# Seven block products in layer 0, a planner that prefers held banks, and layer statistics on ScalarE in a four-layer graph network

## The chip, the cores and the metric

The kernel runs on one core of one Trainium2 chip. The time is the device time of one execution in microseconds. Time before: 1353.37 us, the median of 3 runs (1351.7 to 1353.72). Each run also has a profile of one execution; its span goes from the first to the last instruction of the program.

## The reference

x has 64 samples of 256 nodes with 128 features (fp32), adj is 256 x 256. Four layers follow each other, each with a residual and a layer norm over the features:

```python
x = layernorm(x + L0(x))   # sum over k of adj^k x W_k, k = 0..3 (two equal adjacencies: their weights add)
x = layernorm(x + adj @ (x @ W1) + b1)
x = layernorm(x + norm(adj + I) @ x @ W2.T + b2)
x = layernorm(x + L3(x))   # 5 steps of a gated unit:
#   m = adj @ h;  z = sigmoid(m W34 + h U3);  r = sigmoid(m W4 + h U3)
#   v = tanh(m W5 + (r * h) U5);  h = (1 - z) * h + z * v
```

Layer 0 is folded: with q = a2 x (a2 is adj squared), the layer is x(W0 + I) + q W2 + adj (x W1 + q W3), where W1, W2, W3 are sums of two raw weights each. `w0s` holds these four matrices, centred over the output features so that the layer norm needs no mean.

## The kernel before, in words

Samples go in groups of two (NB = 2), 32 groups in all. A group's tile is 128 x 512: two samples times two halves of the nodes times 128 features. All work is recorded as operations with an engine, a cost, a lag and a rank (the group's number); nothing is issued while recording. `Plan.order` (from L74) then goes through them like a scheduler: on each engine it takes the operation that can start first by these costs, among equals the one of the lowest rank, hands out tile slots ("bank" is one of 8 PSUM banks, "w" an SBUF tile of 128 x 512, and so on) and returns the order. The program is issued in that order, and each engine runs its own queue in order. At most ACTIVE groups (10) are open at a time.

Names that matter for what follows:

- `propagate` multiplies by an adjacency. For all but the first two groups' layer 0 it is `seven` (L590 on): a 2 x 2 block product with 7 instead of 8 products of 128 columns. GpSimd makes differences of the input (ts01, ts2, ts3; L614, L618, L621). TensorE does `first` (one product into quadrant 0), `middle` (three), `more` (one into quadrant 0, after ScalarE has copied that quadrant to `us`, L655) and `rest` (two). VectorE adds up (post11 to post2, L642 to L652).
- `record` (from L732) is a group's whole program. Layer 0: x is loaded; for the first two groups (`near`, HEAD = 4 samples) TensorE transposes it, for the others VectorE transposes 32 x 32 blocks (tx) and two DMAs through DRAM finish it (dx, xT). q comes from `propagate`. Then for each node half `first` does four matmuls of 256 columns (xT by the first two matrices of w0s, or of its row-permuted copy w0p, and qT by the last two), ScalarE copies one half of the bank to v (L771), `second` adds two matmuls of 256 columns with adj, and ScalarE copies the sum out (L783).
- The five steps of layer 3 are `product` calls of 512 columns each: pr (W4 and U3), gate r, r times h on VectorE, ph (W5), pr turned into z's by w34, gate z, ph (U5), gate h, then VectorE's d, e and the new hT, which `packed` sends through DRAM into the other layout (th, dh, h).
- `spread_of` and `normalise_centred` are the layer norm where the mean is zero: ScalarE squares with an accumulated sum (L515), GpSimd adds EPS and takes the power -0.5 (L519, L520), ScalarE scales (L531). `statistics` and `normalise` are layer 3's, with the mean: VectorE's bn_stats and bn_aggr (L491, L495), GpSimd (L501, L502), ScalarE (L551). The last three groups (END = 6 samples) end in `closing` instead, which lets TensorE transpose and centre, and then uses `spread_of`.
- In the set-up, w0_raw becomes w0s (sums on VectorE, then the centring); aTp is adj with its rows interleaved, made by four DMAs (`spread`, L317); `block_sums` (L355 to L359) makes for each adjacency the five block combinations that `seven` needs; p_an is the transpose of the normalised adjacency on TensorE.

All matmuls of these parts go through `mm` at L199, so the profile's groups are told apart by tiles: pmq, pm and pmg are the propagations of layers 0, 1 and 2, and 3; py is layer 0's products and the weights of layers 1 and 2; pr and ph are layer 3's.

Of the kernel before, what the change touches and what calls it, by code (L numbers as in the profile page):

```python
# [13 lines left out]
P = 128  # L14
NB = 2
ACTIVE = 10
# [34 lines left out]
class Plan:  # L51
# [32 lines left out]
    def order(self):  # L84
# [14 lines left out]
        while any(ready.values()):  # L99
            best = None  # L100
            for e, waiting in ready.items():
                t0 = free.get(e, 0.0)
                pick = None
                for at, op in waiting:
                    need = {}
                    for v in placed[op]:
                        if v.slot is None:
                            need[v.kind] = need.get(v.kind, 0) + 1
                    short = False
                    for k, n in need.items():  # L110
                        if len(pool[k]) < n:
                            short = True
                            break
                        at = max(at, sorted(pool[k])[n - 1][0])
                    if short:
                        continue
                    key = (max(at, t0), op.rank, op.seq)
                    if pick is None or key < pick[0]:
                        pick = (key, op)
# [3 lines left out]
            (start, _, _), op = best  # L123
# [34 lines left out]
def kernel(  # L158
# [42 lines left out]
    SHAPES = {"bank": [P, 512], "x": [P, 512], "w": [P, 512], "th": [P, 384], "q": [P, P], "st": [P, Q * 6], "mv": [P, Q * 2],  # L201
              "ve": [P, Q], "rs": [P, Q]}
    slots = {"bank": BANKS, "x": ACTIVE + 3, "w": 48, "th": 10, "q": 10, "dram1": 8, "dram2": 16, "st": 12, "mv": 12, "ve": 24, "rs": 12}
# [18 lines left out]
    def fetch(rank, o, src, v, queue, after=()):  # L222
        e, cost = QUEUES[queue]
        return pre(rank, queue, cost, lambda: e.dma_start(o, src), [], [v], lag=3000, joint=True, after=after)

    def load(rank, name, shape, src, keep=True, queue="SP"):
        v = constant(name, shape) if keep else Val("w", shape, name)
        e, cost = QUEUES[queue]
        pre(rank, queue, cost, lambda: e.dma_start(v.ap, src), [], [v], lag=3000 if queue != "SP" else 2300)
# [5 lines left out]
    nc.vector.memset(half, -0.5)  # L235

# [45 lines left out]
    w0_raw = load(-1, "w0_raw", [P, C, K0], w0)  # L282
# [21 lines left out]
    w0p = constant("w0p", [P, 2, C])  # L304

    def permuted():
        for r in range(4):
            nc.sync.dma_start(w0p.ap.rearrange("(j r) k c -> r j k c", r=4)[r], w0s.ap[32 * r:32 * (r + 1), 0:2, :])

    pre(1.2, "SP", 1800, permuted, [w0s], [w0p])  # L310
# [32 lines left out]
    pre(0.3, "DVE", 600, rows, [ahat, dinv], [ahat])  # L343
    pre(0.3, "PE", 4 * 110, lambda: turn(p_an, ahat), [ahat], [p_an])
# [34 lines left out]
    raw = {name: load(0.6, f"raw_{name}", [P, src.shape[1]], src, False, "SP")  # L379
# [60 lines left out]
    class Group:  # L440
# [44 lines left out]
        def statistics(self, tag, s):  # L485
            st, mv, ve, rs, nm = (self.val(k, n + tag) for k, n in (
                ("st", "st"), ("mv", "mv"), ("ve", "ve"), ("rs", "rs"), ("ve", "nm")))

            def stats():
                for q in range(self.q):  # L490
                    nc.vector.bn_stats(st.ap[:, q * 6:(q + 1) * 6], nat(s)[:, q, :])  # L491

            def aggr():
                for q in range(self.q):
                    nc.vector.bn_aggr(mv.ap[:, 2 * q:2 * q + 2], st.ap[:, q * 6:(q + 1) * 6])  # L495
                mean, var = (mv.ap.rearrange("p (q k) -> p k q", k=2)[:, k] for k in range(2))
                nc.vector.tensor_scalar(ve.ap, var, EPS, None, op0=OP.add)
                nc.vector.tensor_scalar(nm.ap, mean, -1.0, None, op0=OP.mult)

            def scales():  # L500
                nc.gpsimd.tensor_tensor(rs.ap, ve.ap, half[:, :self.q], op=OP.pow)  # L501
                nc.gpsimd.tensor_tensor(mv.ap[:, :self.q], nm.ap, rs.ap, op=OP.mult)  # L502

            self.dve(stats, [s], [st], 195 * self.q)
            self.dve(aggr, [st], [mv, ve, nm], 67 * self.q + 240)
            self.add("POOL", 1300, 100, scales, [ve, nm], [rs, mv])
            return mv, rs

        def spread_of(self, tag, s):
# [3 lines left out]
            def squares():  # L513
                for q in range(self.q):
                    nc.scalar.activation(nat(y)[:, q, :], nat(s)[:, q, :], AF.Square, scale=C ** -0.5,  # L515
                                         accum_out=ve.ap[:, q:q + 1])

            def scales():
                nc.gpsimd.tensor_scalar(ve.ap, ve.ap, EPS, None, op0=OP.add)  # L519
                nc.gpsimd.tensor_tensor(rs.ap, ve.ap, half[:, :self.q], op=OP.pow)  # L520

            self.act(squares, [s], [y, ve], 295 * self.q)
            self.add("POOL", 1330, 100, scales, [ve], [ve, rs])
# [22 lines left out]
        def normalise(self, tag, s, mv, rs):  # L546
            y = self.val("w", "y" + tag)

            def run():
                for q in range(self.q):  # L550
                    nc.scalar.activation(nat(y)[:, q, :], nat(s)[:, q, :], AF.Identity, bias=mv.ap[:, q:q + 1],  # L551
                                         scale=rs.ap[:, q:q + 1])

            self.act(run, [s, mv, rs], [y], 390 * self.q)
            return y

# [36 lines left out]
        def seven(self, tag, h, aTs, ins, blocks):  # L593
# [32 lines left out]
            def first():  # L626
                block(0, ins(h)[:, 0, 0], aTs.ap[:, 0, :P], True)

            def middle():
# [24 lines left out]
            started = self.pe(pe_cost(P, 1), first, [h, aTs], [ps])  # L654
            kept = self.act(lambda: nc.scalar.copy(row(u, 1), row(ps, 0)), [ps], [u], 165)  # L655
# [3 lines left out]
            self.pe(pe_cost(P, 3), middle, [ts, sums], [ps], True, (started,))  # L659
# [39 lines left out]
        def packed(self, name, src):  # L699
# [13 lines left out]
            self.add("SP", 900, 2300, run, [far], [t])  # L713
# [5 lines left out]
        def gate_(self, name, ps, func, bias, kept=True):  # L719

            t = self.val("w", name) if kept else ps
# [10 lines left out]
        def record(self):  # L732
            x_ = self.val("x", "x")
            plan.add("SP", 450, 4500 if self.start < HEAD else 2700, self.rank() - 1.5, lambda: nc.sync.dma_start(nat(x_), self.view(x)), [], [x_],
# [3 lines left out]
            if near:  # L738
                xT, w01 = self.copied("xT", self.transposes("x", x_)), w0s
            else:  # L740

                w01 = w0p
                turn, far = self.val("w", "tx"), self.val("dram", "dx")
                xT = self.val("w", "xT")
                self.dve(lambda: nc.vector.transpose(  # L745
                    turn.ap.rearrange("p (r b i t) -> p r b t i", r=4, t=T, i=32),
                    x_.ap.rearrange("p (b t r j) -> p r b t j", r=4, t=T, j=32)), [x_], [turn])
# [9 lines left out]
            v, s0 = self.val("w", "v"), self.val("w", "s0")  # L757
            py = []

            for t in range(T):  # L760
                p = self.val("bank", f"py0{t}")
                py.append(p)

                def first(p=p, t=t):
                    for b in range(self.nb):
                        o = p.ap[:, b * 2 * C:(b + 1) * 2 * C]
                        mm(o, (tiles if near else pairs)(xT)[:, b, t], w01.ap[:, 0:2, :], b == 0, True, shared=True)
                        mm(o, tiles(qT)[:, b, t], w0s.ap[:, 2:4, :], False, True, shared=True)

                def moved(p=p, t=t):  # L770
                    nc.scalar.copy(parts(v)[:, t], four(p)[:, :, 1, :])  # L771

                self.pe(pe_cost(2 * C, 2 * self.nb), first, [xT, qT, w01, w0s], [p])
                self.act(moved, [p], [v], 55 + 107 * self.nb)
            for t in range(T):

                def second(p=py[t], t=t):
                    for kt in range(T):
                        mm(four(p)[:, :, 0, :], aT.ap[:, kt, t * P:(t + 1) * P], parts(v)[:, kt],
                           False, True, shared=True)  # L780

                def summed(p=py[t], t=t):
                    nc.scalar.copy(nat(s0).rearrange("p (b t) c -> p t b c", t=T)[:, t],  # L783
# [129 lines left out]
```

## Time and profile before

| | |
|---|---|
| median of 3 runs | 1353.37 us (1351.7 to 1353.72) |
| the profiled execution | 1352.22 us, span 1350.3 us |
| granted TensorE clock | 0.999 |
| VectorE's largest group, rh (L729) | 160 of 767 ns |
| ScalarE's squares (L515) | 396 of 299 ns, with 396 accumulator reads of 191 ns |
| GpSimd's power (L520) | 99 of 1052 ns |
| DMA | 134.96 MB, mean 100 GB/s |

A group of the profile names line, engine, operation, output <- input, shapes and count, then busy time, mean of one in ns, the idle time of the engine just before, and what ended it. A wait is given as engine, tile and line, then who was waited for: us in total, times, longest. An ACTIVATE with an accumulated sum stands as two instructions, the second an accumulator read.

### The profile page before, as it was taken

The numbers are of one execution on the slowest core, as the hardware profiler recorded it, in microseconds if no ns is written. First come the engines' busy times: TensorE is split into PE (matmuls) and PEld (weight loads), VectorE is DVE, ScalarE is ACT, GpSimd is POOL, SyncE is SP. The second block draws the span as 40 slices with busy tenths as digits, with TensorE's granted clock in tenths as the row PEclk, the third lists the DMA queues.
The fourth block names the chain that finished last, engine by engine and source line by source line (L and its number), as shares of the span: only waits on it lengthen the run. The fifth ranks groups of instructions, "written<-read, shape, count | busy, mean of one in ns | idle before, by whom it ended". The sixth has DMA issues, their size and how long they took to land.

```text
span 1350.3 us, 22012 instructions
## 1 busy us (share of the span) xinstructions
PE 1336.5 (99%) x6553; PEld 928.3 (69%) x6553; DVE 940.9 (70%) x2304; ACT 758.1 (56%) x2421; POOL 680.7 (50%) x1097
## 2 busy tenths in 40 slices
PE   8999999999999999999999999999999999999997
PEld 7886666676776766677666666676776776565554
DVE  5466677767667667865676776676666677877776
ACT  4675536467654556556565554474655686444445
POOL 5785425266742566247266443383653686233323
PEclk9999999999999999999999999999999999999999
DMA  6322334242522333333233433341332223333323
GB/s 175 109 71 71 94 94 128 77 128 78 147 78 77 111 95 118 115 106 100 64 110 110 127 100 98 94 137 56 110 102 63 82 85 121 87 106 95 93 78 110
DMA packets 269495, 134.96 MB, mean 100 GB/s; under 512 B 175776, under 2 KB 241056, under 8 KB 269376
## 3 DMA queue, kind: packets, MB, share of 16 engines
q1 hardware_dynamic: 269120, 133.42, 34.1%
q8 instruction: 53, 0.87, 0.3%
q14 instruction: 66, 0.54, 0.1%
q0 software_dynamic: 256, 0.13, 0.1%
HBM read 67.31 MB, written 65.80 MB: 99 GB/s over the span
## 4 chain that ended last, share of the span: by engine, by line
PE 95%; DVE 1%; DMA 1%; ACT 1%; issue 0%; SPq 0%; POOLq 0%; ACTq 0%; POOL 0%; DVEq 0%
PE pr L199 31%; PE ph L199 20%; PE pmg L199 19%; PE py L199 15%; PE pm L199 7%; PE pmq L199 3%; DMA x<-in_x_dram 1%; DMA w_raw<-in_L_gnn_weight_dram 0%; PE s L199 0%; DMA dx<-tx 0%; ACT y L515 0%; ACT y L551 0%; DVE s L543 0%; SPq L748 0%; DVE tx L745 0%
## 5 line engine op out<-in xcount | busy, mean ns | idle before, releaser
L199 PE MATMUL pr<-mg,w435u5T 128*128 128x512 f32 x640 | 319.8, 593 | 0.0
L614 POOL TENSOR_TENSOR tsg<-h 128x256 f32<-128x256 f32 x128 | 97.2, 760 | 292.5 <-DMA h<-dh 197.5
L722 ACT ACTIVATE r<-pr,bsum 128x512 f32<-128x512 f32 x160 | 109.7, 685 | 151.5 <-PE pr L199 150.7
L722 ACT ACTIVATE pr<-pr,bsum 128x512 f32<-128x512 f32 x160 | 105.5, 660 | 112.4 <-PE pr L199 109.3
L729 DVE TENSOR_TENSOR rh<-r,hT 128x512 f32<-128x512 f32 x160 | 122.7, 767 | 61.6 <-ACT r L722 60.7
L199 PE MATMUL ph<-rh,w435u5T 128*128 128x512 f32 x320 | 163.6, 594 | 0.0
L199 PE MATMUL ph<-mg,w435u5T 128*128 128x512 f32 x320 | 163.3, 592 | 0.0
L199 PE MATMUL pr<-hT,w2u3T 128*128 128x512 f32 x320 | 163.0, 593 | 0.0
L729 DVE TENSOR_TENSOR d<-ph,hT 128x512 f32<-128x512 f32 x160 | 109.7, 686 | 76.1 <-ACT ph L722 73.0
L199 PEld LDWEIGHTS pr<-mg,w435u5T 128*128 128x128 f32 x640 | 109.4, 191 | 65.3 <-issue 53.3
L722 ACT ACTIVATE ph<-ph,bsum 128x512 f32<-128x512 f32 x160 | 105.6, 660 | 60.4 <-PE ph L199 59.9
L531 ACT ACTIVATE y<-s,rs 128x128 f32<-128x128 f32 x384 | 122.1, 392 | 11.0 <-POOL rs L520 10.7
L515 ACT ACTIVATE y<-s 128x128 f32<-128x128 f32 x396 | 116.7, 299 | 16.9 <-DVE s L538 14.9
L199 PEld LDWEIGHTS pmg<-s_aTp,tsg 128*128 128x128 f32 x768 | 101.8, 192 | 33.5 <-issue 28.5
L652 DVE TENSOR_TENSOR mg<-pmg,usg 128x256 f32<-128x256 f32 x160 | 67.0, 419 | 72.7 <-PE pmg L199 70.4
L199 PEld LDWEIGHTS pmg<-aTp,h 128*128 128x128 f32 x512 | 87.1, 197 | 39.4 <-issue 29.2
L729 DVE TENSOR_TENSOR pr<-pr,d 128x512 f32<-128x512 f32 x157 | 108.7, 692 | 1.5
L520 POOL TENSOR_TENSOR rs<-ve,half 128x4 f32<-128x4 f32 x99 | 104.1, 1052 | 8.3
L519 POOL TENSOR_SCALAR ve<-ve 128x4 f32<-128x4 f32 x99 | 23.2, 234 | 166.6 <-ACT y L515 166.3
L729 DVE TENSOR_TENSOR hT<-hT,pr 128x512 f32<-128x512 f32 x157 | 106.1, 676 | 1.3
L199 PE MATMUL pmg<-s_aTp,tsg 128*128 128x128 f32 x768 | 106.2, 275 | 0.0
L642 DVE TENSOR_TENSOR usg<-usg,pmg 128x128 f32<-128x128 f32 x160 | 45.2, 284 | 81.7 <-PE pmg L199 47.7
(181 smaller groups left out, 2816.9 us busy)
## 6 DMA issues: line engine op xcount, KB each, us to landing
dh<-th SPq DMA_DIRECT2D x160, 256.0 KB, 2.0
h<-dh SPq DMA_DIRECT2D x256, 128.0 KB, 2.5
x<-in_x_dram SPq DMA_DIRECT2D x32, 256.0 KB, 3.4
hT<-dh SPq DMA_DIRECT2D x128, 64.0 KB, 2.0
out_dram<-y SPq DMA_DIRECT2D x32, 256.0 KB, 2.3
dx<-tx SPq DMA_DIRECT2D x30, 256.0 KB, 2.6
xT<-dx SPq DMA_DIRECT2D x60, 128.0 KB, 2.6
dn<-tn SPq DMA_DIRECT2D x29, 256.0 KB, 2.1
```

Source lines behind the costliest of these rows:

```text
L199: nc.tensor.matmul(o, lhsT, rhs, start=start, stop=stop, skip_group_check=shared)
L515: nc.scalar.activation(nat(y)[:, q, :], nat(s)[:, q, :], AF.Square, scale=C ** -0.5, accum_out=ve.ap[:, q:q + 1])
L519: nc.gpsimd.tensor_scalar(ve.ap, ve.ap, EPS, None, op0=OP.add)
L520: nc.gpsimd.tensor_tensor(rs.ap, ve.ap, half[:, :self.q], op=OP.pow)
L531: nc.scalar.mul(nat(y)[:, q, :], nat(s)[:, q, :], rs.ap[:, q:q + 1])
L614: nc.gpsimd.tensor_tensor(ts.ap[:, :2 * P].rearrange("p (x c) -> p x c", x=2), ins(h)[:, 1], ins(h)[:, :, 0], op=OP.subtract)
L642: nc.vector.tensor_tensor(row(u, 0), row(u, 1), row(ps, 3), op=OP.add)
L652: nc.vector.tensor_tensor(o(m, slice(1, 3)), o(ps, slice(1, 3), False), both, op=OP.add)
L722: self.act(lambda: nc.scalar.activation(t.ap, ps.ap, func, bias=bias[1], scale=1.0), [ps, bias[0]], [t], act_cost(self.width) + 100)
L729: self.dve(lambda: nc.vector.tensor_tensor(out(t), way(a), way(b), op=op), [a, b], [t])
```

## The change

Six things change together.

1. Layer 0 of all but the first two groups becomes `inner_seven`. The 2 x 2 block matrix of the four weights is multiplied in 7 block products of 128 columns for each of the two samples (14 matmuls) instead of 8 matmuls of 256 columns. VectorE makes the differences and sums of xT and qT (s1 to s4) and adds up the products (five additions); ScalarE makes one copy (u1) and half of the result. It holds two banks. The weights' combinations w0t are made once on VectorE, and the row-permuted copy w0p with its four DMAs goes. `inner` is the old way, for the first two groups.
2. `Plan.order` gets a second key: among operations that can start at the same time, one that holds a bank already goes before one that does not. ACTIVE becomes 12; "w" slots become 38, "th" and "q" 12, and there are 21 slots of a new kind "h" (128 x 256).
3. Gate r is written to a PSUM bank instead of an SBUF tile.
4. Layer 3's `statistics` go from VectorE to ScalarE: a pass with an accumulated sum, a pass of squares with the negative mean as bias and an accumulated sum; GpSimd makes the scalings.
5. In `spread_of`, EPS enters as a bias of the squares (a 128 x 1 tile `root`) and GpSimd's addition goes.
6. `seven`'s `first` and `middle` become one step `opening` of four products, and the copy of quadrant 0 comes after all four. Costs and lags of loads are set anew, and two set-up steps (rows of ahat, the transpose p_an) get later ranks.

```diff
-ACTIVE = 10
+ACTIVE = 12
...
-                    need = {}
+                    need, opens = {}, 1
                     for v in placed[op]:
                         if v.slot is None:
                             need[v.kind] = need.get(v.kind, 0) + 1
+                        elif v.kind == "bank":
+                            opens = 0
...
-                    key = (max(at, t0), op.rank, op.seq)
+                    key = (max(at, t0), opens, op.rank, op.seq)
...
-    w0_raw = load(-1, "w0_raw", [P, C, K0], w0)
+    w0_raw = load(-1, "w0_raw", [P, C, K0], w0, lag=7300)
...
-    pre(0.3, "DVE", 600, rows, [ahat, dinv], [ahat])
-    pre(0.3, "PE", 4 * 110, lambda: turn(p_an, ahat), [ahat], [p_an])
+    pre(0.9, "DVE", 600, rows, [ahat, dinv, w0s], [ahat])
+    pre(1.1, "PE", 4 * 110, lambda: turn(p_an, ahat), [ahat], [p_an])
...
+            def means():
                 for q in range(self.q):
-                    nc.vector.bn_stats(st.ap[:, q * 6:(q + 1) * 6], nat(s)[:, q, :])
+                    nc.scalar.activation(nat(y)[:, q, :], nat(s)[:, q, :], AF.Identity, accum_out=sums.ap[:, q:q + 1])
...
+            def squares():
                 for q in range(self.q):
-                    nc.vector.bn_aggr(mv.ap[:, 2 * q:2 * q + 2], st.ap[:, q * 6:(q + 1) * 6])
...
+                    nc.scalar.activation(nat(y)[:, q, :], nat(s)[:, q, :], AF.Square, bias=nm.ap[:, q:q + 1],
+                                         accum_out=sums.ap[:, q:q + 1])
...
                     nc.scalar.activation(nat(y)[:, q, :], nat(s)[:, q, :], AF.Square, scale=C ** -0.5,
-                                         accum_out=ve.ap[:, q:q + 1])
+                                         bias=root[:, 0:1], accum_out=ve.ap[:, q:q + 1])
 
             def scales():
-                nc.gpsimd.tensor_scalar(ve.ap, ve.ap, EPS, None, op0=OP.add)
...
+        def inner_seven(self, xT, qT):
...
+            self.add("DVE", 450, 400, s3, [xT], [sd])
+            self.add("DVE", 450, 400, s1, [xT, qT], [ss])
+            self.add("DVE", 450, 400, s2, [xT, ss], [st_])
+            self.add("DVE", 450, 400, s4, [qT, st_], [sf])
+
+            def opening():
+                times(half(out_, 0), at(xT, 0), w0s.ap[:, 0, :], True)
+                times(half(more, 0), whole(st_), w0t.ap[:, 1, :], True)
+                times(half(more, 1), whole(ss), w0t.ap[:, 0, :])
...
+            self.pe(pe_cost(P, 3 * NB), opening, [xT, ss, st_, w0s, w0t], [out_, more])
+            self.act(lambda: nc.scalar.copy(u1.ap, out_.ap[:, :N]), [out_], [u1], 270)
+            self.pe(pe_cost(P, NB), lambda: times(half(out_, 0), at(qT, 0), w0s.ap[:, 2, :]), [qT, w0s], [out_])
+            self.pe(pe_cost(P, NB), lambda: times(half(out_, 1), at(qT, 1), w0t.ap[:, 3, :]), [qT, w0t], [out_])
+            add(lambda: (u2.ap, u1.ap, more.ap[:, :N]), [u1, more], [u2])
+            self.pe(pe_cost(P, NB), lambda: times(half(more, 0), whole(sd), w0t.ap[:, 2, :]), [sd, w0t], [more])
...
+            self.pe(pe_cost(P, NB), lambda: times(half(more, 1), whole(sf), w0s.ap[:, 3, :]), [sf, w0s], [more])
...
-            started = self.pe(pe_cost(P, 1), first, [h, aTs], [ps])
-            kept = self.act(lambda: nc.scalar.copy(row(u, 1), row(ps, 0)), [ps], [u], 165)
             self.add("POOL", 830, 100, ts01, [h], [ts])
             self.add("POOL", 610, 100, ts2, [h, ts], [ts])
             self.add("POOL", 590, 100, ts3, [h, ts], [tq])
-            self.pe(pe_cost(P, 3), middle, [ts, sums], [ps], True, (started,))
+            self.pe(pe_cost(P, 4), opening, [h, ts, aTs, sums], [ps])
+            kept = self.act(lambda: nc.scalar.copy(row(u, 1), row(ps, 0)), [ps], [u], 165)
             self.pe(pe_cost(P, 1), more, [h, aTs], [ps], True, (kept,))
...
-                r = self.gate_(f"r{s}", pr, AF.Sigmoid, rb)
+                r = self.gate_(f"r{s}", pr, AF.Sigmoid, rb, "bank")
```

## The prediction

> **What bounds it now.** I read the page's busy shares first, then the waits of TensorE, then its timeline.
>
> ```profile
> PE 1336.5 (99%) x6553; PEld 928.3 (69%) x6553; DVE 940.9 (70%) x2304; ACT 758.1 (56%) x2421; POOL 680.7 (50%) x1097
> PEclk9999999999999999999999999999999999999999
> PE 95%; DVE 1%; DMA 1%; ACT 1%; issue 0%; SPq 0%; POOLq 0%; ACTq 0%; POOL 0%; DVEq 0%
> ```
>
> TensorE (PE) is busy 99% of the span at the full granted clock, and it is 95% of the chain that ended last. But ends of matmuls are modelled, so "busy" proves little; starts do. This is TensorE's timeline (start, us, line, tiles, shapes, count; an fp32 matmul stands as two instructions):
>
> ```profile
> 705.01 1.02 PE L199 MATMUL pr<-hT,w2u3T 128*128 128x512 f32 x2
> 705.87 1.02 PE L199 MATMUL ph<-mg,w435u5T 128*128 128x512 f32 x2
> 706.72 0.39 PE L199 MATMUL pmg<-aTp,h 128*128 128x128 f32 x2
> 706.95 0.39 PE L199 MATMUL pm<-s_anT,y 128*128 128x128 f32 x2
> 707.17 0.39 PE L199 MATMUL pm<-s_anT,tq 128*128 128x128 f32 x2
> 707.40 0.39 PE L199 MATMUL pm<-s_aT,y 128*128 128x128 f32 x2
> 707.62 0.39 PE L199 MATMUL pm<-s_aT,tq 128*128 128x128 f32 x2
> 707.84 1.03 PE L199 MATMUL py<-v,aT 128*128 128x256 f32 x4
> 708.71 1.02 PE L199 MATMUL pr<-mg,w435u5T 128*128 128x512 f32 x2
> ```
>
> Start to start, an instruction of 512 columns takes 0.43 us (705.01 to 705.87, two of them), one of 256 takes 0.217 (707.84 to 708.71, four), one of 128 takes 0.112 (706.72 to 707.84, ten, each pair with weights of its own). The groups by shape count 1606, 792 and 4155 of them: 690.5 + 171.7 + 466 = 1328 us. The first matmul starts at 1.4 and the last ends at 1343.4, 6.9 before the span does. 1328 + 1.4 + 6.9 = 1336; the other 14 us are matmuls that start later than this pace. So the kernel is one stream of matmuls: what shortens it is fewer columns, fewer late starts, a shorter tail. The late starts that are plain waits:
>
> ```profile
> PE warm L247 <- POOL ident masks.py:199: 1.4, 1, 1.4
> PE pmq L199 <- ACT mq L664: 1.3, 1, 1.3
> PE p_an L259 <- DVE ahat L334: 1.2, 1, 1.2
> PE pm L199 <- DVE m L648: 1.0, 2, 0.7
> PE py L199 <- DVE m L652: 0.6, 1, 0.6
> ```
>
> They and four smaller ones sum to 6.8 us. Adding up over the timeline how far each start lags the pace, 8.2 us of the 14 lie in the first 100 us and 5.4 in the 1240 after them.
>
> **1. The block products of layer 0: -9.7 us.** For 30 of the 32 groups the eight matmuls of 256 columns (16 instructions, py<-w0p,xT and py<-w0s,mq) become fourteen of 128 (28 instructions); the second stage keeps its four of 256. Removed: 30 x 16 x 0.217 = 104.2 us. Added: 30 x 28 x 0.1125 = 94.5 us (0.112 to 0.113 over the run). All of it lies on the stream, so -9.7. The weight loads double, but the same shape already runs 4155 times at 0.112 with a new weight each. The Trainium skill ("TensorE: Matmul & The Clock Gate", section "Wait — 56ns, not 53.3ns?") speaks of a fixed 2.5 ns per matmul beside its columns. By that a 128 would be half of (216.6 - 2.5) plus 2.5 = 109.5 ns, and the saving about 12; the row has 112, and the row decides.
>
> The additions around the products go to VectorE: nine of 256 elements per group (like L652, 0.42 us long, 0.34 apart), 30 x 9 x 0.34 = +92 us, less 29 x 1.2 = 35 for the removed bn_stats and bn_aggr. ScalarE loses two of four copies (0.27 apart, -16). VectorE goes from 70% to about 74%, hidden under TensorE unless it comes late at one place.
>
> **2. Statistics on ScalarE: nothing in the middle, something at the end.** A pair of ACTIVATE and accumulator read is 0.29 apart (L515 at 22.25, 22.54, 22.83). A per-partition operand adds 0.093: y<-s,mv,rs (L551) is 0.385 apart, y<-s,rs (L531) 0.292. So a group's sums cost 4 x 0.29 = 1.17 us, its squares up to 4 x 0.385 = 1.54; 29 x 2.7 = 79 us. The bias that replaces the added EPS in the other 99 normalisations costs at most 396 x 0.093 = 37, and takes 99 x 0.29 from GpSimd, where the new scalings add about 29 x 0.5. ScalarE goes from 56% to some 63%. A square with a bias alone is not in the trace: between 0.29 and 0.385; I take 0.385, the row with a bias.
>
> The gate r kept in PSUM moves ScalarE's write to the form of the in-place gates (660 against 685 ns) and VectorE's read to a PSUM one (d: 686, against rh: 767): gain off the path. The permuted copy of w0 (four DMAs, SP 13.0 to 15.4) goes; SP's next issue waits for VectorE's tx until 21.6 anyway: nothing.
>
> **3. The head: -1.4 us (bounds -3.6 to +2.0).**
>
> ```profile
> 8.23 0.60 PE L674 MATMUL ptx<-ident,x 128*128 128x128 f32 x4
> 10.03 0.81 PE L259 MATMUL p_an<-ident,ahat 128*128 128x128 f32 x4 [1.20 <-DVE ahat L334]
> 10.68 0.60 PE L674 MATMUL ptx<-ident,x 128*128 128x128 f32 x4
> 11.11 3.62 PE L199 MATMUL pmq<-a2T,x 128*128 128x256 f32 x16
> 14.57 0.59 PE L199 MATMUL py<-w0s,xT 128*128 128x256 f32 x2
> ```
>
> p_an moves behind the first layer-0 products, so its 1.5 us of lateness goes. What is late next is w0s: in the changed order VectorE makes the block sums of aT and a2T, then w0's sums, then **the block sums of aTp, and only then centres w0s**. aTp comes by four DMAs issued from 9.2 to 11.1, landing 2.1 to 3.0 later: 13.2 to 14.1. Then 1.07 (the same five instructions at 18.47 to 19.54) and 1.53 (the centring, 10.15 to 11.68): w0s is ready at 15.8 to 16.7, and the products start there, not at 14.57, with p_an's 0.45 still to do: +1.7 to +2.6, I take 2.0. TensorE stands some 3 us there. Against that, behind 14.57 the old head still loses 5.4 (8.2 less 1.5 for p_an and 1.3 at matmuls that run cold at 1 to 8 us, which stay); most are results of x loads that TensorE reaches too soon (the 1.3 at 27.8). TensorE now comes 2 us later, while VectorE's first tx starts at about 19.6 (the centring's end near 16.0 and 3.6 us of small rows), not at 20.9: I keep 2.0 of 5.4. 2.0 - 3.4 = -1.4. Keeping none gives -3.4 (-3.6 with the earliest aTp), keeping all +2.0.
>
> **4. The middle: -0.8 us (bounds -5.4 to +2.1).** 5.4 are lost now. The new order lets a step that already holds a bank go before one that opens one, and has 12 groups open, not 10; that can remove up to all. ScalarE's queue now holds 224 long blocks (squares, scalings); the change adds 58 and lengthens 99 by a third, in all 40% more; if losses go with them, +2.1. Half way, 4.6, is -0.8.
>
> **5. The tail: +2.0 us (bounds +0.7 to +2.6).** VectorE used to take the statistics of the last plain group beside ScalarE. Now ScalarE's last queue is: squares of one group (1.54), sums of group 56 (1.17), gates z and h of group 62, squares 60, a scaling (1.54), squares 56 (1.54), squares 62. The gates used to start at 1339.05 and 1339.90; now at about 1339.75 and 1340.3. Squares 60 end at 1342.4, the scaling at 1343.9, squares 56 at 1345.4, squares 62 at 1346.8, where they ended at 1344.6. GpSimd's last chain is 0.3 shorter, but takes group 56's scaling first: +2.0 net. With no price for the bias +0.7; with TensorE held up by gate h +2.6.
>
> **Sum.** -9.7 - 1.4 - 0.8 + 2.0 = -9.9. The profiled execution took 1352.2 (span 1350.3), inside the runs of 1351.7 to 1353.7 with median 1353.4: 1342.3 by the one, 1343.5 by the other. I say 1342.5. All bounds at once give -18.0 to -3.0; they are unlikely to fall together, and the range stops short below.
>
> **Rivals.** (a) Late starts vanish almost wholly and the head ends at its best: -9.7 - 3.6 - 5 + 1.5 = -17, about 1335. For it: the lags of loads are set nearer to the 4 to 7 us measured. Against: w0s. 6%. (b) ScalarE's queue takes back the gain: in each seven-product step the second matmul on quadrant 0 ("more") must wait until ScalarE has copied that quadrant. The copy takes about 0.2 + 0.27 + 0.1 us after the product. Before, the copy could run beside three further products; now all four come first. In the changed order 84 of 254 such steps have 0.9 us or less of matmuls between, formerly 25: 0.3 us to spare, less than one gate (0.57) or a block of squares (1.5). At 0.1 us lost per each of 84, 1351; **at 0.15 us it decides for slower than before**, at 0.2, 1359. Against: the same tight steps now lose next to nothing (pm <- ACT us, 0.4 in all). 9%, a third of it slower. (c) It doesn't do what it says: narrow products are not cheaper. In the busy column a 128 alone, like pmg<-aTp,h, stands at 99.5 / 512 = 0.194: 28 x 0.194 against 16 x 0.297 is +0.68 per group, +20 in all and 1372. Against: the pace 706.72 to 707.84. 3%.
>
> **The chances.** The forecast has 82%. What a measurement can tell from no change is 0.2%, 2.7 us: below 1350.7 counts as faster. From the forecast 0.80 is faster and 0.02 same, (a) gives 0.06, (b) 0.04 faster, 0.02 same, 0.03 slower, (c) 0.03 slower: 0.90, 0.04, 0.06. The range 1336.5 to 1348.5 takes in bounds of head, middle and tail short of their extremes, and leaves out (a)'s far part, (c) and most of (b).
>
> **What would show it.** Products of layer 0 as 28 instructions of 128 at 0.112; TensorE idle near 13 to 16 us waiting for VectorE's w0s; plain waits behind 100 us at about 5; last squares starting about 2 us after the last matmul. It is wrong if "more" waits on ScalarE's copies add up to over 8 us, or if matmuls lag the pace without a wait.

## The result, and the profile after

The changed kernel took 1345.13 us (median of 4 runs, 1344.37 to 1345.65) against 1353.55 us for the kernel before in the same comparison (4 runs, 1351.7 to 1354.08). The ratio is 0.994, with a 95% interval of 0.9923 to 0.9957. So it is faster by 8.4 us; forecast were 9.9 us and 1342.5. The time lies in the range given (1336.5 to 1348.5).

The profiled execution of the changed kernel took 1345.65 us with a span of 1343.9. It is the slowest of its four, 0.5 above their median, and the profiled execution of before (1352.22) lies 1.3 below its own. Between the two traces there are therefore 6.4 us of span, not 8.4, and the account below is one of 6.4.

From the page of the changed kernel, the busy shares, the granted clock and the chain that ended last:

```profile
PE 1324.9 (99%) x6913; PEld 929.7 (69%) x6913; DVE 1013.8 (75%) x2289; ACT 845.2 (63%) x2825; POOL 648.8 (48%) x1056
...
PEclk9999999999999999999999999999999999999999
...
PE 95%; DVE 2%; ACT 1%; DMA 1%; issue 0%; POOL 0%; SPq 0%; POOLq 0%; DVEq 0%; ACTq 0%
```

Nothing changed in kind. TensorE has 360 instructions more (30 groups times 12) and still fills the span; VectorE went from 70% to 75% and ScalarE from 56% to 63%. TensorE's timeline in the middle, with layer 0's seven products (start, us, line, tiles, shapes, count):

```profile
505.19 0.61 PE L201 MATMUL pz<-w0t,se 128*128 128x128 f32 x4
505.64 0.61 PE L201 MATMUL pz<-w0t,ss 128*128 128x128 f32 x4
506.09 0.39 PE L201 MATMUL pm<-aT,y 128*128 128x128 f32 x2
506.31 0.64 PE L201 MATMUL py<-w0s,xT 128*128 128x128 f32 x4
```

From 505.19 to 506.31 there are ten instructions in 1.12 us: 0.112 each (pz and py<-w0s are layer 0's). This is the pace at which the narrow products were costed. The waits of TensorE, longest first:

```profile
PE py L201 <- DVE w0s L303: 5.1, 1, 5.1
PE pmq L201 <- DVE mq L757: 1.5, 1, 1.5
PE warm L252 <- POOL ident masks.py:199: 1.4, 1, 1.4
PE pm L201 <- ACT us L767: 0.6, 1, 0.6
```

The first is new and is the longest in either of the two traces. It is what the account turns on. I made that account from the start times of all matmuls: the pace is the sum of instructions by shape times their usual distance in that trace (about 0.430, 0.216 and 0.112 us), late is what each start lags behind it, and the tail is what the span goes on after the last matmul ends. The rows add up to 1.7 less than the span, most of it the 1.4 us before the first matmul, the same in both traces. All in us:

| | before | predicted change | after | measured change |
|---|---|---|---|---|
| pace | 1328.1 | -9.7 | 1318.3 | -9.8 |
| late, first 100 us | 8.2 | -1.4 | 13.1 | **+4.9** |
| late, the rest | 5.4 | -0.8 | 1.7 | -3.7 |
| tail | 6.9 | +2.0 | 9.15 | +2.3 |
| span | 1350.3 | -9.9 | 1343.9 | -6.4 |

The products and the tail came as worked out, the middle gave more, and the head took what the middle gave. The head, in TensorE's timeline of the changed kernel:

```profile
10.95 1.89 PE L201 MATMUL pmq<-a2T,x 128*128 128x256 f32 x8
17.90 0.94 PE L201 MATMUL py<-w0s,xT 128*128 128x256 f32 x2 [5.06 <-DVE w0s L303]
18.64 1.06 PE L201 MATMUL py<-w0s,mq 128*128 128x256 f32 x2
...
21.20 0.79 PE L201 MATMUL py<-w0s,xT 128*128 128x256 f32 x2
21.82 0.59 PE L201 MATMUL py<-w0s,mq 128*128 128x256 f32 x2
```

Two things are to be seen. The products start at 17.90, not at 14.57. And from 17.90 to 21.20 the eight instructions of 256 columns take 0.41 us each, while from 21.82 on it is 0.216. The table of stretches says why (length, busy time of each engine, then the granted clock, the DMA share and GB/s):

```profile
14.00:18.00 4.00, 0.10 (x1) 0.13 (x2) 3.31 (x9) 0.00 (x0) 1.49 (x2) 1.00 0.45 133
18.00:22.00 4.00, 4.00 (x11) 3.23 (x12) 3.92 (x10) 0.37 (x1) 2.17 (x5) 0.57 0.00 0
22.00:26.00 4.00, 4.00 (x20) 3.51 (x20) 2.72 (x5) 0.84 (x3) 0.00 (x0) 1.00 0.29 85
```

After five idle microseconds the granted clock is 0.57 over the next four, then 1.00 again. The Trainium skill ("TensorE: Matmul & The Clock Gate", section "What's actually happening") says that TensorE's clock falls to half after at least one idle window of about 3.4 us and comes back after at least one busy window as long. This trace agrees: 5.06 us idle, then 3.3 us at half pace. How idle such a window has to be is read from all the traces in the last section.

VectorE's timeline shows what TensorE waited for:

```profile
9.64 0.39 DVE L292 TENSOR_TENSOR w0s<-w_raw,ident 128x128 f32<-128x128 f32 x1 [0.25 <-DMA w_raw<-in_L_gnn_weight_dram]
9.94 1.00 DVE L294 TENSOR_TENSOR w0s<-w_raw 128x128 f32<-128x128 f32 x3
14.59 0.29 DVE L364 TENSOR_TENSOR s_aTp<-aTp 128x128 f32<-128x128 f32 x1 [3.65 <-DMA aTp<-aT]
...
15.66 0.68 DVE L301 TENSOR_REDUCE w0m<-w0s 128x4 f32<-128x512 f32 x1
...
16.58 1.17 DVE L303 TENSOR_TENSOR w0s<-w0s,w0m 128x512 f32<-128x512 f32 x1
```

The sums of w0s were made at 10.9. The centring (L301 to L303) needs nothing else, but in VectorE's queue it stands behind the block sums of aTp, which is not needed until layer 3 (TensorE first uses it at 107.5). VectorE stands 3.65 us for a load that nobody wants yet.

### The profile page after: what moved, and what is told of

The parts are those of the page before. It is cut to its first block, busy times and chain, and to the rows that moved or that the text cites. A ratio compares the mean times of both kernels' runs of the same rounds, so it can differ in the third digit from the quotient of the medians.

```text
span 1343.9 us, 22953 instructions
## 1 busy us (share of the span) xinstructions
PE 1324.9 (99%) x6913; PEld 929.7 (69%) x6913; DVE 1013.8 (75%) x2289; ACT 845.2 (63%) x2825; POOL 648.8 (48%) x1056
## 4 chain that ended last, share of the span: by engine, by line
PE 95%; DVE 2%; ACT 1%; DMA 1%; issue 0%; POOL 0%; SPq 0%; POOLq 0%; DVEq 0%; ACTq 0%
PE pr L201 30%; PE ph L201 20%; PE pmg L201 19%; PE py L201 11%; PE pm L201 7%; PE pz L201 4%; PE pmq L201 3%; DVE tx L852 0%; DMA x<-in_x_dram 0%; ACT y L559 0%; ACT y L504 0%; ACT y L525 0%; PE warm L252 0%; PE s L201 0%; DMA out_dram<-y 0%
## 5 line engine op out<-in xcount | busy, mean ns | idle before, releaser
L831 ACT ACTIVATE r<-pr,bsum 128x512 f32<-128x512 f32 x160 | 105.1, 657 | 92.9 <-PE pr L201 84.7
L525 ACT ACTIVATE y<-s,root 128x128 f32<-128x128 f32 x396 | 153.7, 393 | 12.5 <-DVE s L547 11.6
L201 PEld LDWEIGHTS pr<-mg,w435u5T 128*128 128x128 f32 x640 | 106.6, 191 | 55.6 <-issue 42.5
L838 DVE TENSOR_TENSOR rh<-r,hT 128x512 f32<-128x512 f32 x160 | 109.2, 683 | 40.6 <-ACT r L831 37.4
L201 PEld LDWEIGHTS pmg<-aTp,h 128*128 128x128 f32 x512 | 91.3, 196 | 66.4 <-issue 39.7
L872 POOL TENSOR_TENSOR yb<-y,wb 128x512 f32<-128x512 f32 x64 | 82.2, 1284 | 39.9 <-ACT y L540 37.9
L201 PE MATMUL pmg<-aTp,h 128*128 128x128 f32 x512 | 99.2, 279 | 0.0
L201 PEld LDWEIGHTS ph<-rh,w435u5T 128*128 128x128 f32 x320 | 57.7, 190 | 57.5 <-issue 42.5
```

The source lines that it names most:

```text
L201: nc.tensor.matmul(o, lhsT, rhs, start=start, stop=stop, skip_group_check=shared)
L831: self.act(lambda: nc.scalar.activation(t.ap, ps.ap, func, bias=bias[1], scale=1.0), [ps, bias[0]], [t], act_cost(self.width) + 100)
L838: self.dve(lambda: nc.vector.tensor_tensor(out(t), way(a), way(b), op=op), [a, b], [t])
L872: nc.gpsimd.tensor_tensor(nat(yb), nat(y), bias[1][:, None, :].to_broadcast([P, self.q, C]), op=OP.add)
```

## The experiments

**Theory.** The net gain is that of the narrow products alone. The other parts cancel: the head loses about 5 because VectorE makes the sums of aTp before it centres w0s, and because the idle time halves TensorE's clock afterwards; the middle gains because the order prefers held banks; the tail loses 2 because ScalarE makes the statistics of the last plain groups. **Rivals:** that the head's lateness comes from the loads and the order as a whole, so that moving one step only moves the wait; that the second key in the order is not what helps the middle; that the time of the kernel is not sensitive to the tail. Kernels named together share a chip and the runs of the kernel before on it: 1354.93 us for e1 to e4, 1354.56 for e0, e5, e8 and e9, 1354.24 for e6, e7, e11 and e12. Compared are the ratios to it.

| run | ratio, 95% interval | pace | late, first 100 | late, rest | tail |
|---|---|---|---|---|---|
| e0, the changed kernel again | 0.9941, 0.9928 to 0.9955 | 1318.3 | 15.3 | 1.4 | 9.2 |
| e1 | 0.9936, 0.9923 to 0.9948 | 1318.3 | 13.9 | 1.4 | 9.15 |
| e2 | 0.9934, 0.9922 to 0.9947 | 1318.3 | 13.6 | 3.0 | 6.6 |
| e3 | 1.0, 0.9991 to 1.0009 | 1327.6 | 12.2 | 1.9 | 9.4 |
| e4 | 0.9939, 0.9926 to 0.9951 | 1322.7 | 9.0 | 1.7 | 9.15 |
| e5 | 1.0066, 1.0053 to 1.0079 | 1318.4 | 14.15 | 20.2 | 6.6 |
| e6 | 0.9968, 0.9956 to 0.9981 | 1318.5 | 14.7 | 4.8 | 9.4 |
| e7 | 0.9941, 0.9928 to 0.9953 | 1318.2 | 14.35 | 3.5 | 7.1 |
| e8 | 0.9907, 0.9893 to 0.992 | 1318.3 | 8.9 | 1.6 | 9.2 |
| e9 | 0.9898, 0.9885 to 0.9912 | 1318.3 | 8.5 | 1.4 | 9.2 |
| e11 | 1.0087, 1.0074 to 1.0101 | 1318.3 | 14.1 | 22.5 | 6.6 |
| e12 | 0.989, 0.9875 to 0.9905 | 1318.3 | 10.65 | 1.7 | 6.8 |

The columns of the account are of one profiled execution each; the head differs by one to two microseconds between executions of the same order (the first product of layer 0 starts at 17.9 in the changed kernel, at 19.0 in e0, at 18.3 in e2).

**e3: eight products again.** Is the gain the products'?

```diff
-            s0 = (self.inner if near else self.inner_seven)(xT, qT)
+            s0 = self.inner(xT, qT)
```

(and `inner` reads xT through the permuted view for the later groups).

> The changed kernel with layer 0 of all groups in the old way: 8 matmuls of 256 columns and 4 with adj, no additions on VectorE; the rest of the change stays. Theory (the gain is columns at the issue pace): 28 instructions of 0.1123 become 16 of 0.216 in 30 groups, +9.5 us of pace, and the late starts stay within 2 us of the changed kernel's: 1353 to 1357. Rival (the gain is the new order of the plan, and the products paid nothing): 1343 to 1348.

The time is that of the kernel before, 1.0 (0.9991 to 1.0009). The pace is 9.3 longer than the changed kernel's, while its late starts and tail stay within a microsecond each. So everything else in the change sums to nothing that can be measured (the interval is 1.2 us to either side), and the products, with their additions on VectorE, carry the whole net gain.

**e1: the sums of aTp right behind the centring.** Is it this one step of VectorE?

```diff
+        ops = plan.order()
+        ops.remove(early_sums)
+        ops.insert(ops.index(centred) + 1, early_sums)
-        for op in plan.order():
+        for op in ops:
```

> The changed kernel, with aTp's block sums issued on VectorE right behind the centring of w0s instead of ahead of it; all else keeps its order. Theory (w0s waits in VectorE's queue behind sums that wait for aTp's DMAs): w0s is ready at about 12.6 us (w_raw lands near 9.7, then 1.3 for its sums and 1.6 for the centring), TensorE's first layer-0 product starts at 13 to 14 instead of 17.9, none of the next eight instructions takes 0.427 us. That is 4 to 5 us of idle and 1.7 us of slow pace, 6; later waits for x loads take back 1 to 4, since VectorE's tx still stand behind the sums: 1340 to 1343. Rival (w_raw's late landing, 9.6 against 8.4, makes w0s late): the first product moves by at most 1 us, 1344 to 1345.5.

The wait for w0s went: in e1's timeline of TensorE the products start at 13.97, at full pace. But the time did not move. A little later, also from its timeline:

```profile
13.97 0.67 PE L201 MATMUL py<-w0s,xT 128*128 128x256 f32 x2
...
34.50 0.76 PE L201 MATMUL pmq<-s_a2T,x 128*128 128x128 f32 x2 [4.98 <-DVE mq L757]
35.05 0.63 PE L201 MATMUL pmq<-s_a2T,tqq 128*128 128x128 f32 x2
```

and VectorE's, which made it wait:

```profile
26.77 1.13 DVE L852 STREAM_TRANSPOSE tx<-x 128x512 f32<-128x512 f32 x1 [2.68 <-DMA x<-in_x_dram]
...
29.94 0.29 DVE L364 TENSOR_TENSOR s_anT<-anT 128x128 f32<-128x128 f32 x1
30.26 1.24 DVE L365 TENSOR_TENSOR s_anT<-s_anT,anT 128x128 f32<-128x128 f32 x1
```

The same five microseconds stand 20 us further on, again with half the pace behind them (the two instructions of 128 columns from 34.50 on take 0.55, where 0.22 is usual). VectorE first stands for a load of x and then makes the block sums of anT, needed only in layer 2, ahead of the additions of q that TensorE wants next. The theory was right on what held w0s and wrong on what its removal is worth: here the first rival's picture held, and the wait moved.

**e8: both block sums later.** The sums of aTp and of anT go behind VectorE's first s1.

```diff
+        place = next(o for o in ops if o.engine == "DVE" and any(v.name == "s1_0" for v in o.vals))
+        for o in (norm_sums, early_sums):
+            ops.remove(o)
+            ops.insert(ops.index(place) + 1, o)
```

> The changed kernel with the block sums of aTp and of the normalised adjacency (anT) both issued on VectorE behind the first addition of layer 1, at about 43 us; TensorE first needs them at 90 and 50. Theory (the head is set by VectorE's queue: once w0s is early, the next wait is for the additions of q behind these sums): TensorE's first product at 13 to 14.5, its wait for mq near 30 us 1 to 2.5 us instead of the 5.0 that the earlier swap left, no half pace behind it, late starts in the first 100 us 7 to 10 us; 2 to 5 us under the changed kernel of this chip. Rival (the x loads alone set the head, the sums are free): late starts stay at 12 to 14, time within 1 us.

Now the gain stays: late starts of the head are 8.9 instead of 15.3 in e0, and the median is 4.5 below e0's on the same chip (1342.04 against 1346.57). The account shows more than the medians, since e0's profiled execution is the slowest of its runs and e8's the fastest. The products start at 12.61:

```profile
12.61 0.67 PE L201 MATMUL py<-w0s,xT 128*128 128x256 f32 x2
13.12 0.59 PE L201 MATMUL py<-w0s,mq 128*128 128x256 f32 x2
```

**e9: e8, and two loads of x earlier.** On SP's queue x_8 and x_10 go ahead of the transfer dx_4.

```diff
+        for n in ("x_10", "x_8"):
+            ops.remove(load[n])
+            ops.insert(ops.index(load["x_6"]) + 1, load[n])
```

> As the last, and the loads of x for groups 8 and 10 issued on SP right behind that of group 6, ahead of the write of tx of group 4, behind which they stand for 8 us in the queue. Theory: their tx no longer stop VectorE for 2.5 us near 24, the additions of q start at about 27, TensorE does not wait near 30 for more than 0.5 us: 1 to 3 us under the last. Rival (landing of the others is pushed back by the two more loads in the air, or TensorE then waits for ScalarE and GpSimd in the same place): within 0.7 us of the last.

1340.89, 1.2 below e8. The four runs of e9 all lie below the four of e8, but the intervals of the ratios overlap and the account has only 0.4 us of it, so the loads' part is likely, not shown. e8 and e9 together show that most of the changed head's lateness was the place of ten small VectorE instructions: with them out of the way the head (8.5) is near before's 8.2.

**e4: TensorE kept busy in the wait.** Is the half pace a consequence of the idle time? Forty transposes into a bank that is free (p_at's) stand between the last product of q and the first of layer 0.

```diff
+            if gap:
+                for i in range(40):
+                    nc.tensor.transpose(p_at.ap[:, (i % 4) * P:(i % 4 + 1) * P], ident, ident)
```

> The changed kernel, with 40 more 128-column transposes into a finished bank issued on TensorE in its wait for w0s (about 4.4 us of work whose result nobody reads). Theory (the first eight instructions behind the wait take 0.427 us instead of 0.216 since TensorE had stood idle for 5 us): the first product still starts at 17.5 to 18.2, all instructions behind it at 0.216: -1.7 us there, part of it taken back by the waits at 34 to 39 us that come of x loads, 1343.4 to 1345. Rival (they are slow because of something else in that place, such as the first use of these weights): they stay at 0.427, 1345 to 1346.

```profile
13.44 4.53 PE L969 MATMUL p_at<-ident 128*128 128x128 f32 x40
19.17 0.67 PE L201 MATMUL py<-w0s,xT 128*128 128x256 f32 x2 [1.20 <-DVE w0s L303]
19.68 0.59 PE L201 MATMUL py<-w0s,mq 128*128 128x256 f32 x2
```

With 1.20 us idle in place of five, every instruction behind it runs at 0.216. So the half pace is paid for standing idle, and the wait costs 1.65 us more than its length (2.2 in e0). The total, expected at 1343.4 to 1345, did not move beyond the noise (1345.94): the products started at 19.17 in this execution, 1.3 later than in the changed kernel's, and the next wait for q's additions was 2.2 us in place of 1.5.

**e2: the last plain groups' statistics back on VectorE.** Groups 54 and 56 (by first sample) use bn_stats and bn_aggr as before.

```diff
+            if 54 <= self.start:
+                return self.vector_statistics(tag, s)
```

> The changed kernel, with the statistics of the last two plain groups (54 and 56) back on VectorE (bn_stats and bn_aggr); order and work of all that comes before stay. Theory (ScalarE's queue of 2.7 us more makes the end late): the last squares start at most 0.3 us after the last matmul instead of 1.7, the span ends 7.0 to 7.6 us after the last matmul instead of 9.15, about 1343.2. Rival (the end is set by GpSimd's power and the output DMA whatever comes before): tail 8.8 to 9.2, 1345.

The tail is 6.6 again, shorter than before's 6.9. But the planner, with other costs, orders the end anew: the squares of closing group 60 stand ahead of the last gate h on ScalarE, that group's output (y) ahead of e on VectorE, and TensorE's last product now waits for e:

```profile
1335.42 1.16 PE L201 MATMUL s<-less,e 128*128 128x128 f32 x8 [1.46 <-DVE e L865]
```

Of the 2.6 us won behind the last matmul, 1.6 are lost ahead of it.

**e7: all statistics back on VectorE.** This undoes one of the three parts that the title names; the planner orders the program anew with it.

```diff
+            if True:
+                return self.vector_statistics(tag, s)
```

> The changed kernel with layer 3's statistics of all groups back on VectorE (bn_stats, bn_aggr), the rest of the change kept. Theory (no engine but TensorE is near its limit, so this move is free in the middle and costs only the tail): late starts behind 100 us stay at 1 to 3 us before the last 30, the tail behind the last matmul is 6.5 to 7.5 us instead of 9.15, a new wait of up to 1.5 near the end as in the run with two groups: 0.5 to 2.5 us under the changed kernel. Rival (VectorE at 75% is the tighter one, and moving statistics off it is what cut the late starts): 4 to 8 us of late starts behind 100 us, 2 to 6 us over the changed kernel.

The ratio is 0.9941, the same as the changed kernel's in e0. The tail falls to 7.1, and the late starts of the rest rise from 1.4 to 3.5. ScalarE's statistics give the middle 2 us and take 2 at the end: their net effect here is nothing that can be measured. Neither theory had both halves.

**e5: the order without its second key.**

```diff
-                    key = (max(at, t0), opens, op.rank, op.seq)
+                    key = (max(at, t0), op.rank, op.seq)
```

> The changed kernel without the planner's new key (a step that holds a bank before one that opens one, among equals). Theory (that key is what cut late starts behind 100 us from 5.4 to 1.7 us): they come back to 4 to 8 us, 1347 to 1351 against 1345. Rival (the wider spacing comes of the split of the block step or of 12 open groups): 1 to 2.5 us behind 100 us, 1344 to 1346.

Slower than the kernel before, 1.0066 (1.0053 to 1.0079). The pace is the same to 0.1 us; late starts behind the first 100 us are 20.2 instead of 1.4. From its list of waits:

```profile
PE s L201 <- DVE e L838: 4.5, 1, 4.5
PE pmg L201 <- ACT usg L767: 2.8, 1, 2.8
```

The 4.5 is in the last group: on ScalarE, statistics, squares and a scaling of other groups stand ahead of and between its last gates. Both are followed by half pace (the eight instructions behind the 4.5 take 2.07 us, against 1.05 in e12). The key is worth 17 us in this program (1363.63 against e0's 1346.57; in the account 18.8 of late starts, less 2.6 of tail and 1.1 of the head). That is nearly twice the products' gain, from one line of the planner.

**e11: without the key, and gate r in SBUF again.** A theory for e5: the key is needed because gate r now holds a bank longer.

```diff
-                key = (max(at, t0), opens, op.rank, op.seq)
+                key = (max(at, t0), op.rank, op.seq)
...
-                r = self.gate_(f"r{s}", pr, AF.Sigmoid, rb, "bank")
+                r = self.gate_(f"r{s}", pr, AF.Sigmoid, rb)
```

> The changed kernel without the new key, and gate r back in an SBUF tile, so that a group holds one bank less in each step. Theory (the key pays for the banks that r and layer 0's second bank take): most of the 20 us of late starts behind 100 us that the key's removal brought go again, 4 to 9 us stay, 1347 to 1353 on this chip. Rival (the key is needed for the products' two banks or the order alone, whatever r does): 15 to 22 us of late starts, 1358 to 1364.

22.5 us of late starts behind the first 100, 1.0087: no better than e5. The theory falls. Which of the new demands makes the old order so poor (two banks for `inner_seven`, twelve groups, the four products of `opening`) stays open.

**e6: ten groups open instead of twelve.**

```diff
-ACTIVE = 12
+ACTIVE = 10
```

> The changed kernel with 10 groups open instead of 12. Theory (the spare groups are what gives TensorE other work when one step is late): late starts behind 100 us rise from 1.7 to 3 to 6 us, 1347 to 1351. Rival (8 banks, not groups, are the limit): 1 to 2.5 us, within 1 us of the changed kernel.

Late starts of the rest are 4.8, near the 5.4 of before, and 0.9968 against 0.9941: two more groups are worth 3 to 4 us. With e5 this says what the middle's gain of 3.7 needs, the other parts being as they are: both the key and the two groups. Whether the four products of `opening` help was not run by itself.

**e12: what the runs pointed to.** e9, with e2's statistics, and with three steps at the end moved: the squares of closing group 60 behind the last gate h on ScalarE, its y behind the last e on VectorE, its closing product behind the last product of layer 3 on TensorE.

```diff
+        last_e = find("DVE", "e_62")[0]
+        behind(find("DVE", "s3_60", "y3_60")[0], last_e)
+        behind(find("ACT", "s3_60", "y3_60")[0], find("ACT", "ph4_62")[0])
+        behind(find("PE", "e_60", "s3_60")[0], find("PE", "rh4_62", "ph4_62")[0])
```

> The version with the block sums of aTp and anT later and the loads of x for groups 8 and 10 earlier, plus the statistics of groups 54 and 56 on VectorE and, at the end, gate h of group 62 ahead of the squares of group 60 on ScalarE, the last e ahead of group 60's result on VectorE. Theory: head as in that version (8.5 us of late starts), no wait for e near the end (the run with two groups on VectorE had 1.5), a tail of 6.6 to 7.2 us: 2 to 3 us under it, 0.987 to 0.989 of the kernel before. Rival (the wait for e only moves): within 1 us of that version.

1339.43, 0.989 (0.9875 to 0.9905): the fastest here, ahead of both kernels. The wait for e is gone and the tail is 6.8; the last product in e12's timeline starts without a wait:

```profile
1331.28 1.05 PE L201 MATMUL s<-less,e 128*128 128x128 f32 x8
```

Against e9 (0.9898) the ratios differ by 0.0008, about 1 us, well inside the intervals. The tail is 2.4 shorter, but the head of the profiled execution is 2.1 later than e9's; that the tail pays in the median is not shown. The head's 2.1 are a wait for VectorE that is 0.7 longer (1.20 against 0.52 in e9) and half pace behind it, some 1.6 us, in TensorE's timeline and in the stretches before and after the clock falls (the granted clock is the third figure from the end):

```profile
34.05 0.81 PE L201 MATMUL pz<-w0t,se 128*128 128x128 f32 x4 [1.20 <-DVE se L649]
34.65 1.06 PE L201 MATMUL pz<-w0t,ss 128*128 128x128 f32 x4
```

```profile
31.11:34.53 3.42, 1.66 (x12) 1.27 (x12) 3.39 (x10) 1.52 (x6) 2.77 (x4) 1.00 0.70 186
34.53:37.94 3.41, 3.41 (x19) 3.41 (x18) 2.92 (x12) 0.00 (x0) 3.41 (x7) 0.50 1.03 290
```

So a wait of 1.20 us, which has no half pace behind it in e4, costs more than twice its length here; the last section says what differs.

## Why the prediction was right, and where it was not

**Products, -9.7: right.** -9.8 in the account, and e3 takes it back alone (9.3). The other price that was weighed there would have given about 12; the pace stayed at 0.112 for 128 columns. Rival (c), narrow products no cheaper, is refuted by the same two numbers.

**The head, -1.4: this step failed.** It measured +4.9 where the bounds ended at +2.0 (by its own latest landing of aTp, with none of the old lateness won back, +2.6). The mechanism was the one named: in the changed order the block sums of aTp stand ahead of the centring of w0s. Its size was wrong in both halves.

- *Up to the first product* (+2.0 taken; measured 17.90 + 0.45 - 14.57 = +3.8). The step put aTp's issues at 9.2 to 11.1, as in the trace of before; they came at 10.5 to 12.3, because SP took 3.66 us over the two issues of raw_u in place of 2.34. It put the centring at 1.53; it took 2.1, its last addition 1.17 in place of 0.69. So "TensorE stands some 3 us there" became 5.06. Why SP took longer stays open.
- *Behind it* (-3.4 taken; measured +1.1). The step held that 5.4 of the old lateness lay behind 14.57. Counted start by start it is 3.8, since the matmuls that run slow from 1 to 7 us are 2.9 late, not 1.3; so a gain of 3.4 was nearly all there was to win. Measured are 4.85: 1.65 are the half pace, of which the step had nothing, and 1.65 a wait for q's additions at 36, the kind that it hoped to lose. e1 shows that such waits follow VectorE's queue, not TensorE's lateness. In that queue the transposes tx are longer than the step knew: x's columns are now read in another order (a part of the diff that the list of the change leaves out; it makes w0p needless), and one takes 1.11 us in place of 0.70. From 22 to 39 us the chain that ended last goes through five of them; at 0.4 each that is at most 2 us, an estimate from these rows. No run puts the old order back, so their part in the head stays open.

In before's trace no half pace stands behind a wait, the longest behind the first matmul being 1.3 us; the matmuls from 1 to 7 us, 0.213 apart in place of 0.112, were the only rows that bore on it, and the step took them as a matter of the start alone. One of the prediction's own signs of being wrong, matmuls that lag the pace without a wait, came here for 1.65 us.

**The middle, -0.8 (bounds -5.4 to +2.1): the right sign, the size too small.** -3.7. The step says half way between its ends, but half way from -5.4 to +2.1 is -1.65, not -0.8; the rows gave no nearer value, and e5 and e6 show that the key and the number of open groups move this term by 3 to 19 us. "Plain waits behind 100 us at about 5" mixed waits with late starts: the late starts there became 1.7, and of the waits a single one of 0.3 is left.

**The tail, +2.0: right.** +2.3, and for the reason given. ScalarE's timeline of the changed kernel at the end, and GpSimd's last two powers with VectorE's last instruction:

```profile
1330.85 0.64 ACT L831 ACTIVATE pr<-pr,bsum 128x512 f32<-128x512 f32 x1
...
1331.99 0.36 ACT L525 ACTIVATE y<-s,root 128x128 f32<-128x128 f32 x1
...
1333.36 1.66 ACT L559 ACTIVATE y<-s,nm,rs 128x128 f32<-128x128 f32 x4
1334.90 0.41 ACT L504 ACTIVATE y<-s,nm 128x128 f32<-128x128 f32 x1
...
1336.43 0.38 ACT L525 ACTIVATE y<-s,root 128x128 f32<-128x128 f32 x1
```

```profile
1336.99 1.01 POOL L509 TENSOR_TENSOR rs<-su,half 128x4 f32<-128x4 f32 x1
...
1338.23 1.01 POOL L529 TENSOR_TENSOR rs<-ve,half 128x4 f32<-128x4 f32 x1
```

```profile
1339.27 0.69 DVE L685 TENSOR_TENSOR y<-s,rs 128x512 f32<-128x512 f32 x1 [3.94 <-POOL rs L529]
```

The last matmul ends at 1334.73 and the last squares start at 1336.43, 1.7 later (2 was said): they queue behind group 56's squares, and the last power then queues, for about 0.3 us, behind group 56's scaling on GpSimd. e2 undoes it, 9.15 to 6.6.

**ScalarE's and VectorE's load: right.** 63% and 75% (63 and 74 were given; the longer tx alone are 30 x 0.41 = 12 us of VectorE, 0.9%). The prices held: sums 0.29 apart (1330.27 to 1330.56 in the same timeline), squares with a bias 0.385 apart, the value taken between 0.29 and 0.385. Rival (b), TensorE waiting at the seven-product step for ScalarE's copies, is refuted: such a wait occurs once, 0.6 us. e7 adds what the prediction did not say: moving the statistics has no net effect that can be measured.

So the time came close partly by luck: two misses have opposite signs, the head 6.3 worse than its step and the middle 2.9 better. Between the traces 3.5 of the 9.9 are missing, between the medians 1.5; the difference is where the two profiled executions lie among their runs.

## What to carry to other kernels

On an engine with an in-order queue, look for the instruction that waits for a load nobody needs yet and see what is queued behind it; put all such steps behind the first consumer chain at once, since moving one alone can merely move the wait (e1 against e8). When TensorE is the bound engine and stands idle for most of some 3.4 us, in one wait or in several, price the slower pace after it as well as the wait. And when several things change together, undo them one at a time: here six parts summed to one part's gain, the statistics that the title names were worth nothing that can be measured, and without one term in a planner's key the loss was larger than all that the arithmetic saved.

## What the runs showed of the hardware

- TensorE's clock falls to half by its share of work in a fixed stretch of time, not by the length of one wait. In all fourteen traces the granted clock is full or half and changes only after whole multiples of 3.41 us. Cut into such stretches, with each instruction counted at its usual distance (twice that at half clock), the traces have 5462 at full clock. The 25 that were filled to less than 0.36 were followed by half clock (13 of them ahead of the last matmul), and the others, filled to 0.38 or more, were not. So 5.06 us idle (the changed kernel, filled to 0.06) and 2.78 (e5, 0.20) were followed by half pace, and so was 1.20 in e12, which shares its stretch with another wait of 0.56 (0.32); 2.49 in e6, split between two stretches filled to 0.59 and 0.62, was not, and neither were 1.20 in e4 and 1.46 in e2. Half clock ended after a stretch filled to 0.91 or more and went on after one of 0.66 or less.
- VectorE's additions of two tensors in SBUF are slower while GpSimd computes. The last addition of the centring took 1.17 us with GpSimd's differences (from 16.49 on) beside it, and 0.69 in e9, where GpSimd had not begun and the DMA engines were about as busy (0.45 and 0.50 of the stretch); an addition of the block sums (L365) took 0.29 us at 14.91 in the changed kernel and 1.24 in e1 beside GpSimd's yb (30.04 to 31.35), though there the DMA engines were also 95% busy. With one input in PSUM this is not so. rh, with r in SBUF before the change, took 0.683 us without GpSimd beside it and 0.831 with it (means of 69 and 91); with r in PSUM after it, 0.683 either way. The Trainium skill ("GPSIMD Engine Reference", section "1. Specifications") says that the two share their interfaces to SBUF, and that VectorE's instructions with two SBUF inputs are among those that contend; these rows agree.
- VectorE's 32 x 32 transposes of x took 1.11 us instead of 0.70 after the change, with the same shape and another order of the input's columns (30 of each, 0.67 to 0.72 and 1.06 to 1.15).
- SP's issues of the same loads varied between the two kernels' traces: raw_w's first 0.43 against 1.64, raw_u's two 3.66 against 2.34. What sets this was not tried.
